# Two convolution layers on one core: rows of layer 1 loaded once, column filtering in a third chunk in a row, and three moved steps

## The chip, the core and the metric

The kernel runs on one core of a Trainium2 chip. The core has a matrix engine (PE), a vector engine (DVE), an activation engine (ACT), a general engine (POOL) and an engine that only issues transfers (SP). Each engine works through its own list of instructions in order; transfers between HBM and on-chip memory run on 16 DMA engines beside them. The metric is the device time of one execution in microseconds (us), the median of several runs. A change of up to 0.2% is taken as none.

## The reference

The input x has 8 images of 32 channels and 252 x 252 pixels, all float32. Two layers of the same form follow each other: a group normalization with 16 groups of two channels, a 5 x 5 convolution from 32 to 32 channels with reflected borders, and a residual sum. The reference writes the convolution as a product of Fourier transforms; with these paddings it is the plain convolution of the padded image.

```python
def _gn(v, G=16, eps=1e-5):
    B_, C_, H_, W_ = v.shape
    g = v.reshape(B_, G, C_ // G, H_, W_)
    m = jnp.mean(g, axis=(2, 3, 4), keepdims=True)
    s = jnp.var(g, axis=(2, 3, 4), keepdims=True)
    return ((g - m) / jnp.sqrt(s + eps)).reshape(v.shape)
...
x = x + _L0_conv_ref(_gn(x), L0_conv_weight)
x = x + _L1_conv_ref(_gn(x), L1_conv_weight)
```

## The kernel before

**Layout.** The 128 partitions hold 4 x 32: two column parities times two row parities of an image, times the 32 channels. A 5 x 5 convolution on the image is then a 3 x 3 convolution from 128 to 128 channels on an image of a quarter of the size. An image is cut into 8 chunks of 16 of these rows. The texts name a chunk (b, l, c): image, layer index (0 is layer 1, 1 is layer 2) and chunk. The normalization's scale is folded into the weights and its mean into a bias.

**Filtering.** Along the rows the kernel uses a filtering scheme with six points for four output rows. `transform` (L533) forms the points on DVE from sums and differences of rows: `row_pairs` (v, L562), `row_quads` (u, L571 and 572), `last_rows` (L578 and 579), then `point2` (L587), `point4` (L591), `point1` (L597), `point3` (L594) and `points05` (L604). In layer 2, `row_sums` (L544) gets v by DMA instead: POOL issues a copy (L552) and, when it has landed, two transfers that add to it (L554, L555). `conv` (L656) then multiplies: points 2 and 4 into the PSUM tiles m, points 1 and 3 into pairs (seeded by ACT from m, L724 and 726), points 0 and 5 into sums. Each product is three matmuls, one for each column of the 3 x 3 filter (L680). DVE and ACT combine the results to output rows: `evacuate` (L732), `difference` (L743), `inner` (L752, 753), `parts05` (L758, 759) and `outer` (L780).

**Column chunks.** In some chunks (`by_columns`, L961) points 0 and 5 are also filtered along the columns. DVE prepares sums and differences of columns (`columns`, L607: L613, L614, then L617 in layer 1 or L622 and 623 in layer 2), PE does eight short products instead of twelve passes of full length (`column_product`, L702, with a half-scaled copy L706 by ACT in between), and DVE puts the parts together (`column_parts`, L787 to 789).

**Order.** The chunks of layer 1 of image b + 1 alternate with those of layer 2 of image b (`order`, L946); image 0 begins alone and layer 2 of image 7 ends alone. Nothing is scheduled at run time: every step is entered in a table with a time of a hand-made clock, and each engine's list is the table in order of these times. `begin(i)` is the time at which chunk i starts on PE; a chunk takes 10.2 for its first four points, and `own` and `late` tell how much of points 0 and 5 is done in it and how much in the next. The times only set the order; waits are by semaphores.

**Loads.** `load` (L132, issued by SP) fetches the 16 rows of a layer-1 chunk into xs, in four quarters of 32 partitions. The two quarters of the other column parity hold the same pixels shifted by one. Where `once` (L161) holds, only two quarters are loaded, in two parts (2 rows and 14 rows), and `even_columns` (L156, at L159) copies them to the other half of the partitions, by ACT. `borders` (L145) fills the reflected columns on POOL: L148, 153 and 154, or L148, 150 and 151 where `once` holds. xs has two buffers. `once` holds in ten chunks: seven of image 0 and three of image 1.

**Rest.** ACT also forms the sums for the next image's statistics (`piece_sums`, L231 and 237) and the squares for layer 2's (`squares`, L855). `finish_stats` (L386) turns sums to scale factors by way of `variance` (L369, 371) and `inverse` (L377 to 383); `scale_points` (L511, ACT) and `add_residual` (L479, POOL) prepare the weights. `store` (L909) interleaves output columns into o (L917, by ACT, or by DVE in the last but one chunk) and `send_rows` (L896) lets SP write them; `store_half` (L930) does the last chunk.

Of the kernel before, what the change touches and what calls it, by code (L numbers as in the profile page):

```python
# [42 lines left out]
F32 = mybir.dt.float32  # L43
# [6 lines left out]
P = 128  # L50
# [6 lines left out]
def tile_conv_preact_x2(ctx: ExitStack, tc: tile.TileContext, x: bass.AP, w0: bass.AP, w1: bass.AP, out: bass.AP):  # L57
    nc = tc.nc
    B, C, H, W = x.shape
# [4 lines left out]
    ROWS = 4 * NT  # L64
    NCH = 8
    WIN = (NB + 2, NB + 3)
    WOUT = (NB, NB + 1)
# [8 lines left out]
    spool = ctx.enter_context(tc.tile_pool(name="spool", bufs=2))  # L76
# [15 lines left out]
    def at(t: float, fn, *args, **kw):  # L92
        table.append((t, len(table), fn, args, kw))
# [66 lines left out]

    def once(b: int, c: int) -> bool:  # L161

        return c < (NCH - 1, 3)[b] if b < 2 else False

    def parts(b: int, c: int):

        if once(b, c):
            return ((0, 10), (10, 6)) if (b, c) == (0, 0) else ((0, 2), (2, 14))
        return ((0, ROWS),) + (((ROWS, 2),) if c == NCH - 1 else ())
# [363 lines left out]
    def transform(t0: float, t1: float, b: int, l: int, c: int, free: float = -100.0, now=(0, 0, 0)):  # L533

        wi = WIN[l]
        got = {}

        def source():
            if l == 0:
# [4 lines left out]
        def row_sums(add: bool):  # L544

            t, nxt = source()
            if not add:

                i = max(order.index((b, l, c)) - order.index((B - 2, 1, NCH - 2)), 1 if (b, c) == (0, 1) else 0)
                got["v"] = vpool.tile([P, ROWS, wi], F32, tag=("va", "v")[i % 2], name=f"v_{b}_{l}_{c}")  # L550
                got["vt"] = got["v"].rearrange("p (t i) w -> p t i w", i=4)
                G.dma_start(got["v"], t)  # L552
            else:
                G.dma_start(got["v"][:, 0 : ROWS - 2], t[:, 2:ROWS], accum_op=ALU.add)  # L554
                G.dma_start(got["v"][:, ROWS - 2 : ROWS], nxt[:, 0:2], accum_op=ALU.add)  # L555

        def row_pairs(j0: int = 0, j1: int = NT):
            if j0 == 0:
                got["v"] = vpool.tile([P, ROWS, wi], F32, tag="v", name=f"v_{b}_{l}_{c}")
            v, (t, nxt) = got["v"], source()  # L560
            r0, r1 = 4 * j0, min(4 * j1, ROWS - 2)
            V.tensor_sub(v[:, r0:r1], t[:, r0 + 2 : r1 + 2], t[:, r0:r1])  # L562
            got["vt"] = v.rearrange("p (t i) w -> p t i w", i=4)

        def row_quads(j0: int = 0, j1: int = NT):
# [8 lines left out]
        def last_rows():  # L574

            u2, (t, nxt) = got["u"][:, 1], source()
            if l == 0:
                V.tensor_sub(got["v"][:, ROWS - 2 : ROWS], nxt[:, 0:2], t[:, ROWS - 2 : ROWS])  # L578
# [47 lines left out]
        if (b, l, c) == order[0]:  # L626
            at(t0 - 33.3, row_quads, 0, 2)
            at(t0 - 31, point2, 0, 2)
            for fn in (row_pairs, point4):
                at(t0, fn, 0, 2)  # L630
            at(t0 + 0.2, row_quads, 2, 4)
            at(t0 + 0.2, row_pairs, 2, 4)
            at(t0 + 0.2, last_rows)
            at(t0 + 0.2, point2, 2, 4)
            at(t0 + 0.2, point4, 2, 4)
            at(t0 + 4.9, point1)
            at(t0 + 5.5, point3)
            at(t0 + 6.2, points05)
        else:
            if l:  # L640
                two = begin(order.index((b, l, c)) - 2)
                at(two + 1.45, row_sums, False)
                at(two + 8.4, row_sums, True)
            else:
                at(t0, row_pairs)
            for dt, fn in ((2, row_quads), (3.2, last_rows), (3.6, point2)):
                at(t0 + dt, fn)
            at(max(t0 + 4.2, free + 9.45) if l else t0 + 4.2, point4)
# [244 lines left out]
        at(times[2], reflect)  # L893


    def send_rows(b: int, c: int, h: int, s: int, got):  # L896
        o = got["o"]
        for rp in range(2):
            r = 2 * (c * ROWS + 8 * h + 4 * s) - 1 + rp
            use = [i for i in range(4) if 0 <= r + 2 * i < H]  # L900
            if not use:
                continue
            i, m = use[0], len(use)
            q = 2 * s + rp
            S.dma_start(
                out[b, :, r + 2 * i : r + 2 * i + 2 * m - 1 : 2, :], o[q * Q : (q + 1) * Q, i : i + m, 1 : 1 + W]
            )

    def store(t0: float, b: int, c: int, got):  # L909
        copy = V.tensor_copy if (b, c) == (B - 1, NCH - 2) else A.copy  # L910

        def interleave(h: int, s: int):
            if s == 0:
                got["o", h] = opool.tile([P, 4, 2 * WOUT[1]], F32, tag="o", name=f"o_{b}_{c}_{h}")
            r, m = 8 * h + 4 * s, (3 if (c, h, s) == (NCH - 1, 1, 1) else 4)
            for cp in range(2):
                copy(got["o", h][halves[s], 0:m, cp::2], got["y"][halves[cp], r : r + m, :])  # L917

        def send(h: int):
            got["o"] = got.pop(("o", h))  # L920
            for s in range(2):
                send_rows(b, c, h, s, got)

        for i, t in enumerate((0, 3.3, 5.8, 7.8)):
            at(t0 + t, interleave, i // 2, i % 2)
        at(t0 + 4.6, send, 0)
        at(t0 + 9.1, send, 1)


    def store_half(t0: float, b: int, c: int, h: int, got):  # L930
        def interleave(s: int, rows: slice, engines):
            if (s, rows.start) == (0, 1):
                got["o"] = opool.tile([P, 4, 2 * WOUT[1]], F32, tag="o", name=f"o_{b}_{c}_{h}")
            for cp in range(2):
                dst, src = got["o"][halves[s], rows, cp::2], got["y"][halves[cp], 4 * s : 4 * s + 4][:, rows]
                eng = engines[cp]
                (eng.copy if eng is A else eng.tensor_copy)(dst, src)

        for s in range(2):
            eng = (A, A) if h or not s else (V, V)  # L940
            at(t0 - 0.2, interleave, s, slice(1, 3), eng)
            at(t0 + 1.4, interleave, s, slice(0, 1) if h and s else slice(0, 4, 3), (A, V) if h else eng)
            at(t0 + 1.4, send_rows, b, c, h, s, got)


    order = [(0, 0, c) for c in range(NCH)]  # L946
# [81 lines left out]
    for i, (b, l, c) in enumerate(order):  # L1028
# [11 lines left out]
        if i + 1 < len(order):  # L1040
            transform(t0 + (6.3 if i == 0 else 2.9), t1 + 0.2, *order[i + 1], free=t0, now=(b, l, c))
            nb, nl, ncx = order[i + 1]
            k = inputs.index((nb, ncx)) + 2
            if nl == 0 and 2 < k < len(inputs):
                for part in parts(*inputs[k]):
# [3 lines left out]
                    if once(*inputs[k]):  # L1049
                        kb, kc = inputs[k]  # L1050
                        t = 5.25 if part[0] == 0 and (kb, kc) != (1, 0) else 13.55 if kb else 8.5
                        at(t1 + t, even_columns, *inputs[k], *part)
# [71 lines left out]
```

## Time and profile before

| what | value |
|---|---|
| time, median of 3 runs | 1893.33 us (1890.24 to 1894.27) |
| the profiled execution: time, span | 1893.14 us, 1891.4 us |
| granted PE clock, mean | 0.994 |
| DMA queues: SP's (q1), POOL's (q0) | 272.09 MB, 135.28 MB |
| DMA share in 229 us of the middle (709 to 938 us) | 0.97 |
| DVE busy in the same 229 us | 213.05 us |
| ACT busy in the same 229 us | 178.36 us |

The profile comes from one execution, so sums are made against 1893.14 us. A group's row gives line, engine, operation, output and inputs, shape, the count, then busy time and mean ns of one, and behind the last bar the idle time of the engine just before these instructions with what ended it. A timeline row gives start and length in us, and in brackets the idle time before it. PEld is PE's weight load, which overlaps its matmuls.

### The profile page before, as it was taken

The page shows a single profiled execution, that of the slowest core. Times are in us where ns is not written, and L with a number is a line of the kernel's source. Part 1 is how long each engine was busy: PE and PEld are TensorE (multiplying, and loading weights), DVE is VectorE, ACT ScalarE, POOL GpSimd, SP SyncE. Part 2 cuts the span into 40 slices and gives each one's busy share as a digit, 9 for nine tenths or more (in the row PEclk, how much of TensorE's full clock was granted, in tenths as well). Part 3 has the DMA queues.
Part 4 walks back from the last instruction along what each step waited for, and adds up shares of the span by engine and source line. Part 5 has one row for each costly group of instructions (what it writes and reads, how often), then busy time and mean ns, then how long its engine had stood idle before and what let it go on. Part 6 is the DMA issues. An engine that isn't in the chain of part 4 may idle for free.

```text
span 1891.4 us, 20043 instructions
## 1 busy us (share of the span) xinstructions
PE 1851.5 (98%) x5162; PEld 956.7 (51%) x5162; DVE 1698.0 (90%) x2972; ACT 1401.1 (74%) x2695; POOL 372.9 (20%) x733
## 2 busy tenths in 40 slices
PE   5999999999999999999999999999999999999997
PEld 4444455545555555544555455555555545554455
DVE  7987899999998999999899898999989999998685
ACT  5887678778777787778787687877787765565665
POOL 4543211120112210131111310113111131111210
PEclk8999999999999999999999999999999999999999
DMA  9887899999999999999999989999999978995785
GB/s 278 205 176 191 201 248 230 212 229 253 219 239 239 206 249 233 212 244 219 246 224 229 220 214 258 221 227 226 215 260 220 236 184 177 193 203 145 192 217 113
DMA packets 248627, 411.41 MB, mean 218 GB/s; under 512 B 19520, under 2 KB 215488, under 8 KB 238144
## 3 DMA queue, kind: packets, MB, share of 16 engines
q1 hardware_dynamic: 220384, 272.09, 61.8%
q0 software_dynamic: 27648, 135.28, 28.7%
q10 hardware_dynamic: 480, 2.77, 0.4%
q8 instruction: 41, 0.67, 0.2%
q14 instruction: 74, 0.61, 0.1%
HBM read 207.41 MB, written 67.39 MB: 145 GB/s over the span
## 4 chain that ended last, share of the span: by engine, by line
PE 76%; DVE 9%; DMA 8%; ACT 3%; issue 2%; POOL 1%; SPq 0%; DVEq 0%; ACTq 0%; POOLq 0%
PE m L680 27%; PE pairs L680 26%; PE sums L680 8%; PE sums L702 6%; PE extra L702 6%; DMA v<-y 4%; PE extra L680 4%; DMA st<-in_x_dram 1%; DMA xs<-in_x_dram 1%; DMA out_dram<-o 1%; DVE sd L743 1%; ACT o L917 1%; DMA v<-ytail 1%; DVE t L604 1%; POOL u L479 0%
## 5 line engine op out<-in xcount | busy, mean ns | idle before, releaser
L680 PE MATMUL pairs<-t,u 128*128 128x504 f32 (+2 forms) x1548 | 690.4, 585 | 2.7 <-ACT pairs L726 1.6
L680 PE MATMUL m<-t,u 128*128 128x508 f32 (+3 forms) x1560 | 675.2, 581 | 7.1 <-DVE t L591 2.6
L680 PEld LDWEIGHTS m<-t,u 128*128 128x128 f32 x1560 | 293.3, 189 | 325.6 <-issue 297.4
L680 PEld LDWEIGHTS pairs<-t,u 128*128 128x128 f32 x1548 | 289.2, 189 | 321.5 <-issue 295.6
L917 ACT COPY o<-y 64x508 f32<-64x508 f32 x496 | 327.2, 660 | 8.9 <-DMA out_dram<-o 0.2
L743 DVE SCALAR_TENSOR_TENSOR sd<-sd,pairs 128x504 f32<-128x504 f32 (+2 forms) x258 | 163.9, 670 | 19.2 <-PE pairs L680 16.0
L680 PE MATMUL sums<-t,u 128*128 128x508 f32 (+5 forms) x408 | 175.3, 578 | 0.0
L855 ACT ACTIVATE junk<-y,negk 128x1008 bf16<-128x1008 f32 (+1 forms) x144 | 147.4, 1024 | 30.6 <-PE extra L702 14.9
L726 ACT COPY pairs<-m 128x504 f32<-128x504 f32 (+1 forms) x129 | 72.5, 562 | 129.6 <-PE m L680 110.0
L732 ACT COPY sd<-m 128x504 f32<-128x504 f32 (+2 forms) x258 | 137.0, 583 | 32.0 <-DVE sums L789 24.7
L604 DVE SCALAR_TENSOR_TENSOR t<-v 128x1024 f32<-128x1024 f32 (+1 forms) x128 | 157.5, 1230 | 3.5 <-PE sums L680 3.5
L702 PE MATMUL extra<-sdiff,wc 128*128 128x252 f32 (+3 forms) x616 | 156.3, 375 | 3.3 <-ACT extra L706 2.6
L702 PEld LDWEIGHTS extra<-sdiff,wc 128*128 128x128 f32 x616 | 113.5, 188 | 89.6 <-issue 50.2
L591 DVE SCALAR_TENSOR_TENSOR t<-v 128x512 f32<-128x512 f32 (+2 forms) x129 | 89.7, 695 | 65.6 <-DMA v<-y 47.7
L702 PE MATMUL sums<-d,u 128*128 128x252 f32 (+3 forms) x616 | 142.3, 373 | 0.0
L562 DVE TENSOR_TENSOR v<-xs 128x1792 f32<-128x1792 f32 (+1 forms) x65 | 129.5, 1993 | 1.8 <-issue 0.7
L554 POOL DMA_DIRECT2D v<-y x64 | 55.2, 863 | 377.7 <-DMA v<-y 377.7
L702 PEld LDWEIGHTS sums<-d,u 128*128 128x128 f32 x616 | 115.3, 189 | 26.9 <-issue 11.8
L237 ACT ACTIVATE st<-st,negk 128x1134 f32<-128x1134 f32 x98 | 121.7, 1242 | 3.2
L148 POOL COPY xs<-xs 64x32 f32<-64x32 f32 (+3 forms) x74 | 34.1, 461 | 450.2 <-DMA xs<-in_x_dram 330.7
L680 PEld LDWEIGHTS sums<-t,u 128*128 128x128 f32 x408 | 75.9, 188 | 80.1 <-issue 77.2
L231 ACT ACTIVATE st<-st 128x1134 f32<-128x1134 f32 x98 | 112.2, 1145 | 4.0 <-DMA st<-in_x_dram 2.8
(171 smaller groups left out, 2424.7 us busy)
## 6 DMA issues: line engine op xcount, KB each, us to landing
xs<-in_x_dram SPq DMA_DIRECT2D x176, 504.0 KB, 12.6
v<-y POOLq DMA_DIRECT2D x64, 1032.0 KB, 5.7
st<-in_x_dram SPq DMA_DIRECT2D x111, 567.0 KB, 6.9
out_dram<-o SPq DMA_DIRECT2D x488, 126.0 KB, 5.7
v<-y POOLq DMA_DIRECT2D x64, 903.0 KB, 9.9
u<-ud SPq DMA_DIRECT2D x15, 1152.0 KB, 5.6
xs<-in_x_dram SPq DMA_DIRECT2D x30, 441.0 KB, 6.7
xs<-in_x_dram SPq DMA_DIRECT2D x28, 472.5 KB, 11.1
```

The costliest lines, as they stand in the source:

```text
L231: A.activation(junk, src, AF.Identity, accum_out=acc[:, 0, i : i + 1])
L237: A.activation(junk, src, AF.Square, bias=negk, accum_out=acc[:, 1, i : i + 1])
L562: V.tensor_sub(v[:, r0:r1], t[:, r0 + 2 : r1 + 2], t[:, r0:r1])
L591: stt(ts[b, l, c][0][:, 1, j0:j1], vt[:, :, 1], -2.0, vt[:, :, 2], ALU.mult, ALU.add)
L604: stt(t, got["vt"][:, :, 0:2], 4.0 if l else -4.0, got["vt"][:, :, 2:4], ALU.mult, ALU.add)
L680: T.matmul(dst, u[:, k, 2 - i, :], rhs[:, j0 + i0 : j0 + i1, i : i + wo], start=(i == 0 and not add), stop=(i == 2), skip_group_check=add,)
L702: T.matmul(dst[:, 0, use], w, rhs[:, use], start=(i == 2), stop=True, skip_group_check=(i != 2))
L726: A.copy(dst, src)
L732: A.copy(got["sd"][:, 1 + e], m24[e][:, 0:n])
L743: stt(d, d, -2.0, pairs13[e][:, 0:n], ALU.mult, ALU.add)
L855: A.activation(dst, src, AF.Square, bias=negk, scale=1.0 if i else -1.0, accum_out=acc[:, 1, at_ : at_ + 1])
L917: copy(got["o", h][halves[s], 0:m, cp::2], got["y"][halves[cp], r : r + m, :])
```

## The change

There are five edits.

1. **Loads.** `once` holds in all chunks of layer 1 but the last of each image and chunk 1 (chunk 3 in image 1). The new ones are marked by `copied_late`: their two parts are loaded at the old place, and the borders and copies of the two parts have later times of their own. One copy of image 1 moves from 13.55 to 20.
2. **Columns.** `by_columns` takes chunk 2 of layer 2 in images 0 to 6 and chunk 3 in image 7.
3. **First chunk of layer 2.** (0, 1, 0) forms its v on DVE, as layer 1 does, with sums for differences. Only the later chunks of layer 2 use the transfers that add.
4. **Statistics of the last image.** `variance` and `inverse` of its layer 2 move from 12.82 and 13.55 to 11.3 and 12.5.
5. **The end.** o of the last but one chunk is taken from the pool of the statistics' pieces, and POOL issues its sends. Two sends of the last half chunk go to ACT's queue.

```diff
     def once(b: int, c: int) -> bool:
-        return c < (NCH - 1, 3)[b] if b < 2 else False
+        return c != NCH - 1 and (c != 1 if b > 1 else c != 3 if b else True)
+
+    def copied_late(b: int, c: int) -> bool:
+        return once(b, c) and (b > 1 or (b == 1 and c > 3))
...
+        sent = l == 1 and (b, c) != (0, 0)
...
-                i = max(order.index((b, l, c)) - order.index((B - 2, 1, NCH - 2)), 1 if (b, c) == (0, 1) else 0)
+                i = max(order.index((b, l, c)) - order.index((B - 2, 1, NCH - 2)), 0)
...
-            V.tensor_sub(v[:, r0:r1], t[:, r0 + 2 : r1 + 2], t[:, r0:r1])
+            (V.tensor_add if l else V.tensor_sub)(v[:, r0:r1], t[:, r0 + 2 : r1 + 2], t[:, r0:r1])
...
-            if l:
+            if sent:
                 two = begin(order.index((b, l, c)) - 2)
                 at(two + 1.45, row_sums, False)
                 at(two + 8.4, row_sums, True)
...
-            S.dma_start(
+            engines[rp].dma_start(
...
+        end = (b, c) == (B - 1, NCH - 2)
+        copy = V.tensor_copy if end else A.copy
...
-                got["o", h] = opool.tile([P, 4, 2 * WOUT[1]], F32, tag="o", name=f"o_{b}_{c}_{h}")
+                pool, tag = (spool, "st") if end else (opool, "o")
+                got["o", h] = pool.tile([P, 4, 2 * WOUT[1]], F32, tag=tag, name=f"o_{b}_{c}_{h}")
...
-                send_rows(b, c, h, s, got)
+                send_rows(b, c, h, s, got, (G, G) if end else (S, S))
...
-            at(t0 + 1.4, send_rows, b, c, h, s, got)
+            at(t0 + 1.4, send_rows, b, c, h, s, got, (S, A) if h and s else (S, S))
...
-        return c in {B - 1: (1, 2, 4, 5), B - 2: (1, 3)}.get(b, (1, 3, 5, 7))
+        return c in {B - 1: (1, 2, 3, 4, 5), B - 2: (1, 2, 3)}.get(b, (1, 2, 3, 5, 7))
...
+                    if copied_late(kb, kc):
+                        at(t0 + 9.5, load, kb, kc, *part)
+                        at(begin(i + 2) + 4.0 if part[0] else t1 + 5.5, borders, kb, kc, *part)
+                        at(begin(i + 3) + 4.0 if part[0] else t1 + 9.35, even_columns, kb, kc, *part)
+                        continue
...
-                        t = 5.25 if part[0] == 0 and (kb, kc) != (1, 0) else 13.55 if kb else 8.5
+                        t = 5.25 if part[0] == 0 and (kb, kc) != (1, 0) else (20.0 if kc == 2 else 13.55) if kb else 8.5
...
-            finish_stats(b, 1, *(te + t for t in (3.0 if b < B - 1 else 4.4, 6.85, 6.86, 10.25 if b else 9.9, 12.82, 13.55)))
+            finish_stats(b, 1, *(te + t for t in (3.0 if b < B - 1 else 4.4, 6.85, 6.86, 10.25 if b else 9.9, *((12.82, 13.55) if b < B - 1 else (11.3, 12.5)))))
```

More of the change, by code (lines that the diff above doesn't have):

```diff
@@ L576, in last_rows @@
             u2, (t, nxt) = got["u"][:, 1], source()
-            if l == 0:
-                V.tensor_sub(got["v"][:, ROWS - 2 : ROWS], nxt[:, 0:2], t[:, ROWS - 2 : ROWS])
+            if not sent:
+                (V.tensor_add if l else V.tensor_sub)(got["v"][:, ROWS - 2 : ROWS], nxt[:, 0:2], t[:, ROWS - 2 : ROWS])
             stt(u2[:, NT - 1], t[:, ROWS - 2], 4.0 if l else -4.0, nxt[:, 0], ALU.mult, ALU.add)
@@ L647, in transform @@
                 at(t0 + dt, fn)
-            at(max(t0 + 4.2, free + 9.45) if l else t0 + 4.2, point4)
+            at(max(t0 + 4.2, free + 9.45) if sent else t0 + 4.2, point4)
             at(max(t0 + 5.5, free + 7.8), point1)
@@ L893, in keep, with send_rows @@
         at(times[2], reflect)
-    def send_rows(b: int, c: int, h: int, s: int, got):
+    def send_rows(b: int, c: int, h: int, s: int, got, engines):
         o = got["o"]
@@ L909, in store @@
     def store(t0: float, b: int, c: int, got):
-        copy = V.tensor_copy if (b, c) == (B - 1, NCH - 2) else A.copy
+        end = (b, c) == (B - 1, NCH - 2)
+        copy = V.tensor_copy if end else A.copy
         def interleave(h: int, s: int):
             if s == 0:
-                got["o", h] = opool.tile([P, 4, 2 * WOUT[1]], F32, tag="o", name=f"o_{b}_{c}_{h}")
+                pool, tag = (spool, "st") if end else (opool, "o")
+                got["o", h] = pool.tile([P, 4, 2 * WOUT[1]], F32, tag=tag, name=f"o_{b}_{c}_{h}")
             r, m = 8 * h + 4 * s, (3 if (c, h, s) == (NCH - 1, 1, 1) else 4)
@@ L1044, in tile_conv_preact_x2 @@
             if nl == 0 and 2 < k < len(inputs):
-                for part in parts(*inputs[k]):
+                kb, kc = inputs[k]
+                for part in parts(kb, kc):
+                    if copied_late(kb, kc):
[3 more added lines that the diff above has]
+                        continue
                     early = once(*inputs[k]) or nb == 0
@@ L1048, in tile_conv_preact_x2 @@
                     at(t1 + (0.2 if early else 9.0), borders, *inputs[k], *part)
-                    if once(*inputs[k]):
-                        kb, kc = inputs[k]
-                        t = 5.25 if part[0] == 0 and (kb, kc) != (1, 0) else 13.55 if kb else 8.5
-                        at(t1 + t, even_columns, *inputs[k], *part)
+                    if once(kb, kc):
+                        t = 5.25 if part[0] == 0 and (kb, kc) != (1, 0) else (20.0 if kc == 2 else 13.55) if kb else 8.5
+                        at(t1 + t, even_columns, kb, kc, *part)
         if c == 0 and any(by_columns(b, l, k) for k in range(NCH)):
```

## The prediction

> **What bounds the kernel now.** I read the page's busy shares first, then its costliest groups, then the timeline.
>
> ```profile
> PE 1851.5 (98%) x5162; PEld 956.7 (51%) x5162; DVE 1698.0 (90%) x2972; ACT 1401.1 (74%) x2695; POOL 372.9 (20%) x733
> PEclk8999999999999999999999999999999999999999
> L680 PE MATMUL pairs<-t,u 128*128 128x504 f32 (+2 forms) x1548 | 690.4, 585 | 2.7 <-ACT pairs L726 1.6
> L680 PE MATMUL m<-t,u 128*128 128x508 f32 (+3 forms) x1560 | 675.2, 581 | 7.1 <-DVE t L591 2.6
> ```
>
> PE is busy 98% at full clock, and its two largest groups waited 10 us in all. Is it at its rate? [...]
>
> ```profile
> 904.36 5.23 PE L680 MATMUL m<-t,u 128*128 128x504 f32 x12
> 905.21 0.19 PEld L680 LDWEIGHTS m<-t,u 128*128 128x128 f32 x1 [0.23 <-issue]
> 905.63 0.19 PEld L680 LDWEIGHTS m<-t,u 128*128 128x128 f32 x1 [0.23 <-issue]
> 911.44 1.20 DVE L617 TENSOR_TENSOR d<-t 128x1008 f32<-128x1008 f32 x1
> 917.91 5.27 PE L680 MATMUL m<-t,u 128*128 128x508 f32 x12
> 929.85 5.23 PE L680 MATMUL m<-t,u 128*128 128x504 f32 x12
> ...
> 944.00 0.70 DVE L591 SCALAR_TENSOR_TENSOR t<-v 128x516 f32<-128x516 f32 x1 [4.20 <-DMA v<-y]
> 967.63 0.68 DVE L614 TENSOR_TENSOR sdiff<-t 128x504 f32<-128x504 f32 x1
> ```
>
> A weight load goes out every 0.42 us, which is what one pass of a matmul streams; the idle 0.23 us ends by "issue", not by data. [...] The same starts check the code's own clock: chunk (4,0,2) lasts 13.55, the plain (3,1,2) 11.94 with 3.4 us of its work put off into the next. By `own` and `late` (L966) a column chunk costs 13.6, a plain one 15.3, and between image edges the starts keep to this within 0.1 us. PE's schedule is the kernel's time; DVE is the near second. It has no idle over 0.2 us between 904 and 929, then 4.20 waiting for v.
>
> **Columns in eight more chunks.** `by_columns` gains chunk 2 of layer 2 in images 0 to 6 and chunk 3 in image 7. PE gains 15.3 - 13.6 = 1.7 each, **13.6 us**. DVE pays, start to start: columns (L613, 614, 622, 623) 2.52, column_parts (L787 to 789) 1.89, less 0.22 since the sums go to SBUF and not PSUM: +4.19. ACT pays one L706, 0.58, in a chunk that grows by 1.7.
>
> Is there room on DVE? Chunks 1, 2, 3 of layer 2 now stand in a row with layer-1 column chunks between. The tight consumer is the second half of PE's chunk, which reads sdiff (L614). In chunk (5,0,0), start 1077.08, L614 ended at 1085.81 and PE's extra matmul started at 1085.86 after 0.17 idle: the deadline is +8.61 us from a chunk's start. L614 of (4,0,2) ends at 911.53, +7.17. From there to L614 of (4,0,4), end 968.31, DVE takes 56.78; without the 4.20 wait and with 4.19 more work, 56.77. PE covers these four chunks in 54.41 instead of 56.11. So L614 lands at 7.17 + 56.77 - 54.41 = +9.53, **0.92 late**. The same sum on the other images (waits for v of 2.0 to 4.5 there) gives 0.8, 0.6, 0.9, 0.9, 0.9, 1.1 and, for image 6, whose L614 starts from +8.5, 2.0: 7.2 us. After that comes a plain chunk and the 3 us idle of chunk 5, so it is paid once per image. In image 7 no layer-1 work is beside it; L614 ends at +4.5 there and the 1.7 stays whole. Net **-6.4**.
>
> Is the v wait really free? v of (3,1,3) landed at 944.00, 26.1 after the start of (3,1,2). With the added work DVE reaches L591 at about +26.1 too, so the wait goes, and with fewer loads v should be no later.
>
> **Rows loaded once.** `once` grows from 10 chunks to 49. Each of the 39 drops two DMAs of 504 KB, some 40 of 411 MB. That brings no time directly: what waits for DMA is DVE,
>
> ```profile
> DVE t L591 <- DMA v<-y: 47.7, 17, 10.6
> ```
>
> and apart from the handover below PE does not wait behind it. The relief pays for the columns only. ACT gets two copies each (L159): 64x256, 0.42, and 64x1792, 1.86: 39 x 2.28 = 89 us. The long one is due at +4.0 of a layer-1 chunk. There ACT idles 1.88 us between its two seeds (L724 ends 907.75, L726 starts 909.63, waiting for PE), so the copy fits; L726 is 0.1 late, and its seed is used only at +7.65. The short one, +9.35, comes behind the L706 that PE waits for, in a chunk with 3.9 us of ACT idle. Behind both on ACT stand evacuations with over 1 us to spare. **0**; if the gap is missed, see the second rival. On SP the number of DMAs is the same and the loads keep their place. POOL's borders go from 3 copies a chunk to 6, at places where L552 has gone and the load, 12.6 us from issue, has landed.
>
> [...]
>
> ```profile
> L571 DVE SCALAR_TENSOR_TENSOR u<-y x64: 689/696/727, 176.1 to 1853.8; 128x516 f32<-128x516 f32 x64
> L151 POOL COPY xs<-xs x20: 179/202/2014, 30.2 to 164.6; 64x2 f32<-64x2 f32 x9, 64x14 f32<-64x14 f32 x9, 64x10 f32<-64x10 f32 x1, 64x6 f32<-64x6 f32 x1
> ```
>
> None lost more than 31 ns, while a 0.2 us POOL copy took up to 2.0: POOL is the one that waits. [...] I take 0.02 x 6 x 7 = **+0.8**.
>
> **Repairs.** Three stalls of PE stand in the trace.
>
> ```profile
> 189.62 0.70 DVE L591 SCALAR_TENSOR_TENSOR t<-v 128x516 f32<-128x516 f32 x1 [10.59 <-DMA v<-y]
> 190.46 2.79 PE L680 MATMUL m<-t,u 128*128 128x508 f32 x6 [2.05 <-DVE t L591]
> ...
> 1747.31 0.15 DVE L369 TENSOR_SCALAR var<-m 128x1 f32<-128x1 f32 x1
> 1747.52 3.67 PE L680 MATMUL m<-t,u 128*128 128x508 f32 x8 [2.08 <-DVE var L369]
> ...
> 1881.89 0.85 DVE L917 COPY o<-y 64x508 f32<-64x508 f32 x2 [4.25 <-DMA out_dram<-o]
> ```
>
> Chunk (0,1,0) takes its row sums on DVE. The 2.05 goes, and a 0.23 wait in the same chunk. But the 2.0 us row_pairs (L562, mean 1.993) is due at +2.9 of the chunk before, between var and inverse (+3.35), so rstd is ready at 178.0 instead of 176.2. The scaling L511 then starts 0.9 later (L159, moved from +13.55 to +20, no longer stands before it), and the seed L726 behind it with it: PE's wait of 1.38 at 178.61 grows by about 0.95. Net **-1.3**, between -2.3 and 0.
>
> In the last image's statistics var moves from 12.82 to 11.3, ahead of L743's second half, which waits for PE: it can run at 1742.9, when its matmul (1742.49) is done. The 2.08 goes: **-2.1**; nothing is late next, since inverse follows at 12.5 before L594.
>
> At the end, o of the last but one chunk comes from a free pool. L917 runs at 1877.7, not 1881.9. Then L743 waits for the pairs matmuls (end 1880.44) instead: L743 1881.0, L752 and L753 1881.7, the fourth L917 1882.6, L758 and L759 1883.3, L766 1883.9, L937 1884.6 against 1886.97. From there to the span's end took 4.4. The sends on POOL's queue are not in the trace: at L555's 1.2 us each, four after 1882.6 are issued by 1887.4 and land perhaps 2 later, about even with the last store. Bounds 0 to -3; I take **-2.0**.
>
> Sum: -6.4 + 0.8 - 1.3 - 2.1 - 2.0 = -11.0. The profiled execution took 1893.14 (span 1891.4); its 1882.1 is against the median 1893.33, 0.2 higher: **1882 us**. No change means within 0.2%, about 1889.5 to 1897.1, what this measurement can tell.
>
> **Rivals.** *No stall in the three chunks* (17%): DVE gets through, as its rows run a little faster with fewer POOL waits and transfers beside it; then 13.6 + 5.4 come whole: 1874. For it: 0.9 us late is 1.6% of 56.8. Against it: L613 to L623 do not wait for memory now.
>
> *The copies delay the seeds* (15%): if borders, queued on POOL behind L552's wait for L604, end late, the 1.86 us copy moves right. L726 with 0.6 must be done at +7.65, so the copy must start by +5.2, 1.8 after its gap opens. From 2.1 late it costs 0.28 in each of 39, 11 us in all, and the time is 1893, no change. Against it: POOL has a whole chunk of 13 us before that.
>
> [...]
>
> The forecast's own case, 1877 to 1888, has 50%; 9% lies between it and no change. The range 1873 to 1891 takes in the first rival and half of the way to the second. Faster 0.76, same 0.15, slower 0.09.
>
> **What would show it.** PE's chunk starts 13.6 apart through chunks 1 to 3; in chunk 4 a PE wait of 0.6 to 1.1 us before the extra matmuls, ended by DVE L614; L591's wait for v gone there; ACT's L726 still at +5.3; DMA share down by a tenth; no L591 wait near 189, no L369 wait near 1735; L917 without the DMA wait. Wrong would be PE waits ended by L726 in every layer-1 chunk, or L571 rows longer by tenths of a us.

## The result and the profile after

The changed kernel takes 1879.19 us (median of 4 runs, 1878.92 to 1884.91) against 1893.8 for the kernel before beside it (4 runs, 1890.24 to 1895.86): a ratio of 0.993, 95% interval 0.9915 to 0.9945. The forecast was 1882 with a range of 1873 to 1891. The profiled executions have spans of 1891.4 and 1877.5 us, 13.9 apart, where the forecast's sum was 11.0. The sum came near, but several of its terms did not: part of its nearness is luck, since errors of opposite sign made up for each other (below).

In the changed kernel's code the lines stand a little lower: L591 is now L596, L604 L609, L614 L619, L680 L685, L702 L707, L706 L711, L724 and 726 are L729 and 731, L917 is L925, L905 (the send inside `send_rows`) L910. The page after, the busy shares and PE's two largest groups:

```profile
PE 1839.2 (98%) x5194; PEld 966.0 (51%) x5194; DVE 1731.2 (92%) x3030; ACT 1493.8 (80%) x2781; POOL 396.2 (21%) x855
L685 PE MATMUL pairs<-t,u 128*128 128x504 f32 (+2 forms) x1548 | 692.9, 586 | 5.4 <-ACT pairs L729 3.3
L685 PE MATMUL m<-t,u 128*128 128x508 f32 (+3 forms) x1560 | 674.8, 581 | 3.4 <-DVE u L526 1.9
```

PE is busy 12.3 us less and still 98% of the span; DVE has 33 us more work and ACT 93. PE's waits moved from DVE (L591, var) to ACT (L729). POOL's queue moved 134.20 MB, 1.1 less than before (the first chunk of layer 2 no longer uses it for v), SP's 230.73 instead of 272.09.

The stretch that the forecast worked out, image 3's three column chunks, is here, from the timeline (start, length, idle before it). Chunk (4,0,1) starts at 871.43, (4,0,2) at 902.05, (4,0,4) at 956.50; L596 adds v into the fourth point, and L619 makes the sdiff that PE's extra products (L707) read:

```profile
883.58 0.70 DVE L596 SCALAR_TENSOR_TENSOR t<-v 128x516 f32<-128x516 f32 x1
907.41 0.68 DVE L619 TENSOR_TENSOR sdiff<-t 128x504 f32<-128x504 f32 x1
910.51 1.01 PE L707 MATMUL extra<-sdiff,wc 128*128 128x252 f32 x4
963.93 0.68 DVE L619 TENSOR_TENSOR sdiff<-t 128x504 f32<-128x504 f32 x1
964.95 0.37 PE L707 MATMUL extra<-sdiff,wc 128*128 128x252 f32 x1
```

L619 of (4,0,2) ends 6.04 after its chunk's start, and that of (4,0,4) at +8.11, half a microsecond before the +8.61 that the forecast gave as the deadline. PE does not wait. The kernel before, at the first two of these places (its chunk (4,0,1) starts at 873.74, (4,0,2) at 904.36):

```profile
887.21 0.70 DVE L591 SCALAR_TENSOR_TENSOR t<-v 128x516 f32<-128x516 f32 x1 [1.46 <-DMA v<-y]
910.85 0.68 DVE L614 TENSOR_TENSOR sdiff<-t 128x504 f32<-128x504 f32 x1
```

Before, DVE waited 1.46 us for v one chunk ahead of the stretch, and L614 ended at +7.17. That wait is gone after the change, and the three chunks begin 1.1 us earlier on DVE. Its cause is what the experiments were for.

To see where the 13.9 us came from, each chunk's start on PE is set against the code's own clock, and the lag's growth is read by stretch:

| part | forecast | measured |
|---|---|---|
| PE's own work, eight chunks, by the code's clock | -13.6 | -13.6 |
| stalls in the three column chunks | +7.2 | +0.8, all in image 0 |
| POOL's added copies, as time lost by DVE | +0.8 | not seen |
| handover, from the start of (1,0,0) to that of (0,1,2) | -1.3 | +0.6 (+2.4 in two other profiles) |
| var of the last image | -2.1 | -1.4 |
| the end, from the last chunk's start | -2.0 | -0.1 |
| the start, up to PE's first chunk | | +0.8 |
| turns from one image to the next | | -1.0 |
| sum | -11.0 | -13.9 |

The lag is how much later a chunk starts than the code's clock has it. Over the three column chunks of the changed kernel it stays within 0.05 us in images 1 to 6, which is how PE's own work is measured; the other rows are the change of the lag. Each profile is one execution. The turns cost 0.7 to 3.6 us an image over the profiles of this study (run 7 below aside), and which of them are long differs from one profile to the next; a difference of 2 us between two profiles means nothing by itself. The handover took 5.4 us before and 6.0 here, but 7.8 in runs 6 and 9 below, which have the same steps in this place: one profile each does not settle the size of this row.

### The profile page after: what moved, and what is told of

Same layout as the page of the kernel before. It is cut to its first block, busy times and chain, and to the rows that moved or that the text cites. A ratio compares the mean times of both kernels' runs of the same rounds, so it can differ in the third digit from the quotient of the medians.

```text
span 1877.5 us, 20381 instructions
## 1 busy us (share of the span) xinstructions
PE 1839.2 (98%) x5194; PEld 966.0 (51%) x5194; DVE 1731.2 (92%) x3030; ACT 1493.8 (80%) x2781; POOL 396.2 (21%) x855
## 2 busy tenths in 40 slices
DMA packets 207110, 369.07 MB, mean 197 GB/s; under 512 B 19088, under 2 KB 173968, under 8 KB 196752
## 3 DMA queue, kind: packets, MB, share of 16 engines
q1 hardware_dynamic: 178832, 230.73, 49.8%
q0 software_dynamic: 27600, 134.20, 29.3%
## 4 chain that ended last, share of the span: by engine, by line
PE 80%; DVE 7%; DMA 6%; ACT 3%; issue 3%; SPq 0%; POOL 0%; DVEq 0%; ACTq 0%; POOLq 0%
PE m L685 28%; PE pairs L685 28%; PE sums L707 7%; PE extra L707 6%; PE sums L685 6%; PE extra L685 4%; DMA v<-y 2%; DMA st<-in_x_dram 1%; DMA v<-ytail 1%; DMA xs<-in_x_dram 1%; ACT o L925 1%; DVE sd L748 1%; DVE t L609 1%; DMA wraw<-in_L_conv_weight_dram 1%; DMA out_dram<-o 0%
## 5 line engine op out<-in xcount | busy, mean ns | idle before, releaser
L685 PE MATMUL pairs<-t,u 128*128 128x504 f32 (+2 forms) x1548 | 692.9, 586 | 5.4 <-ACT pairs L729 3.3
L685 PE MATMUL m<-t,u 128*128 128x508 f32 (+3 forms) x1560 | 674.8, 581 | 3.4 <-DVE u L526 1.9
L685 PEld LDWEIGHTS m<-t,u 128*128 128x128 f32 x1560 | 294.2, 189 | 317.1 <-issue 297.0
L685 PEld LDWEIGHTS pairs<-t,u 128*128 128x128 f32 x1548 | 290.2, 189 | 320.1 <-issue 289.1
L925 ACT COPY o<-y 64x508 f32<-64x508 f32 x496 | 327.5, 660 | 8.6
L707 PEld LDWEIGHTS extra<-sdiff,wc 128*128 128x128 f32 x680 | 125.9, 189 | 98.1 <-issue 47.8
L707 PE MATMUL extra<-sdiff,wc 128*128 128x252 f32 (+3 forms) x680 | 173.0, 376 | 3.4 <-ACT extra L711 2.3
L557 POOL DMA_DIRECT2D v<-y x63 | 35.7, 567 | 622.7 <-DVE t L609 608.4
L609 DVE SCALAR_TENSOR_TENSOR t<-v 128x1024 f32<-128x1024 f32 (+1 forms) x128 | 157.7, 1232 | 5.4 <-PE sums L685 5.4
L707 PE MATMUL sums<-d,u 128*128 128x252 f32 (+3 forms) x680 | 157.4, 374 | 0.0
L707 PEld LDWEIGHTS sums<-d,u 128*128 128x128 f32 x680 | 127.6, 189 | 24.9 <-issue 9.0
L685 PE MATMUL sums<-t,u 128*128 128x508 f32 (+5 forms) x312 | 133.6, 577 | 0.0
L559 POOL DMA_DIRECT2D v<-y x63 | 54.3, 862 | 329.1 <-DMA v<-y 329.1
L159 ACT COPY xs<-xs 64x1792 f32<-64x1792 f32 (+2 forms) x97 | 109.3, 1129 | 13.4 <-POOL xs L151 11.1
L729 ACT ACTIVATE pairs<-m,means 128x504 f32<-128x504 f32 (+1 forms) x129 | 84.2, 653 | 44.5 <-PE m L685 36.0
L785 ACT ACTIVATE y<-sums 128x504 f32<-128x504 f32 (+1 forms) x158 | 94.5, 634 | 28.3 <-PE sums L707 19.2
L235 ACT ACTIVATE st<-st 128x1134 f32<-128x1134 f32 x98 | 112.5, 1148 | 5.0 <-DMA st<-in_x_dram 3.2
```

The source lines that it names most:

```text
L159: copy(t[64:128, :, 0:256:2], t[0:64, :, 1:256:2])
L235: A.activation(junk, src, AF.Identity, accum_out=acc[:, 0, i : i + 1])
L609: stt(t, got["vt"][:, :, 0:2], 4.0 if l else -4.0, got["vt"][:, :, 2:4], ALU.mult, ALU.add)
L685: T.matmul(dst, u[:, k, 2 - i, :], rhs[:, j0 + i0 : j0 + i1, i : i + wo], start=(i == 0 and not add), stop=(i == 2), skip_group_check=add,)
L707: T.matmul(dst[:, 0, use], w, rhs[:, use], start=(i == 2), stop=True, skip_group_check=(i != 2))
L785: A.activation(y, src, AF.Copy, scale=1.0 - 2 * i, **total(3 * i))
```

## The experiments

Each run's ratio is to the kernel before, timed on the same chip beside it (median 1894.46, 1893.76, 1892.56 and 1892.68 in the four groups).

**1. Columns alone.** Only `by_columns` is changed.

```diff
-        return c in {B - 1: (1, 2, 4, 5), B - 2: (1, 3)}.get(b, (1, 3, 5, 7))
+        return c in {B - 1: (1, 2, 3, 4, 5), B - 2: (1, 2, 3)}.get(b, (1, 2, 3, 5, 7))
```

> The kernel before with the column edit alone; loads, first chunk, statistics and end as before. Theory (the loads make the room): DVE enters the stretch of chunks 1 to 3 with the wait for v of chunk (b,1,1) still there (1.5 us at 886 us in the trace of before), so L614 of chunk 4 ends at about +9.5 us from its chunk's start, past +8.6, and PE waits 0.6 to 1.0 us before the extra matmuls in nearly every image: 5 to 7 us in all, and the time is 1885 to 1888. Rival (DVE had the room anyway, the forecast only mis-added): L614 at about +8.1, no waits, the whole 13.6 us come and the time is about 1880.

1890.97 us, ratio 0.9983 (0.9969 to 0.9998), 3.5 us faster by the median; 1885 to 1888 was expected, and only four of its ten runs (1886.34 to 1895.83), the profiled one among them, lie there. Its timeline in the same stretch (SPq and POOL rows are issues of transfers; chunks (4,0,1), (4,0,2), (4,0,4) start at 872.00, 902.78, 957.83):

```profile
870.49 2.26 SPq L143 DMA_DIRECT2D xs<-in_x_dram  x4
871.28 0.86 POOL L554 DMA_DIRECT2D v<-y  x1 [5.40 <-DMA v<-y]
885.83 0.69 DVE L591 SCALAR_TENSOR_TENSOR t<-v 128x516 f32<-128x516 f32 x1 [1.38 <-DMA v<-y]
909.48 0.68 DVE L614 TENSOR_TENSOR sdiff<-t 128x504 f32<-128x504 f32 x1
966.75 1.12 PE L702 MATMUL extra<-sdiff,wc 128*128 128x252 f32 x4 [0.31 <-DVE sdiff L614]
```

Here the forecast's picture is true: the wait for v stands, L614 of (4,0,2) ends at +7.38, and PE waits for L614 in (4,0,4) at +8.92. Over the three column chunks the lag grows by 0.8, 1.5, 1.2, 1.2, 1.3, 1.1 and 1.5 in images 0 to 6, 8.5 us where the forecast had 7.2; where the forecast put it all in (b+1,0,4), some of it falls in the chunk ahead. So the stall exists, and something else in the change takes it away.

**2. Loads alone.** `once`, `copied_late` and their loads, borders and copies; columns and repairs as before.

> The kernel before with the load edit alone (39 more chunks loaded once and copied by ACT, with their late borders and copies). Theory: no time for itself, within 2 us of before, while DVE's wait for v (L591, 47.7 us before) falls below 30 us and vanishes in chunk 1 of layer 1. Rival 1 (the copies cost ACT): slower by 2 us or more, PE waits ended by the seeds. Rival 2 (the lighter load cures the waits at image edges, 2.4 us of PE time in two of them before): faster by 2 to 3 us.

1891.35 us, 0.9986 (0.9975 to 0.9997). It brings some 3 us by the median, where none had been expected; its profiled execution took 1893.21, as long as that of the kernel before, so the trace does not say where they lie. What matters here it does show ((4,0,2) starts at 904.95):

```profile
886.53 0.69 DVE L596 SCALAR_TENSOR_TENSOR t<-v 128x516 f32<-128x516 f32 x1
910.32 0.68 DVE L619 TENSOR_TENSOR sdiff<-t 128x504 f32<-128x504 f32 x1
```

The wait for v in (4,0,1) is gone, and sdiff of (4,0,2) ends at +6.05.

**3. Repairs alone.** The row sums of (0,1,0) on DVE, the last image's statistics, the end.

> The kernel before with the three repairs alone (v of the first chunk of layer 2 on DVE, earlier variance of the last image, another buffer and other queues at the end). The forecast: -5.4 us, so 1888. From the trace after the change I now expect less: the first -1.3 becomes about +0.6, the second -1.4, the third -0.2, some -1 us in all, so 1892 to 1893, with PE's weight loads 0.84 us apart for a few us after its idle stretch in chunk (1,0,1).

1893.37 us, 0.9993 (0.9976 to 1.0009): no difference that this measurement can tell. The forecast gave these three 5.4.

**4. All, with the full bytes.** The changed kernel, but the late-copied chunks load all four quarters.

```diff
-        for cp, rp in quads[: 2 if once(b, c) else 4]:
+        for cp, rp in quads[: 2 if once(b, c) and not copied_late(b, c) else 4]:
```

> The changed kernel, but the late-copied chunks load all four quarters again, the other half being overwritten by ACT's copy with the same values. ACT, POOL and DVE do what they do after the change; only the 40 MB are back. Theory (bytes, not copies, decide when v lands and so whether DVE has room): the wait for v in chunk 1 returns with 1 to 2 us, L619 of chunk 4 ends past +8.6, PE waits 4 to 7 us more in all, time 1883 to 1886. Rival: as after the change, 1879.

1883.65 us, 0.9945 (0.9925 to 0.9964), with 409.34 MB instead of 369.07. The time lies within the 1883 to 1886 that was expected if bytes decide, but not for that reason: in images 1 to 6 the three chunks keep their start at +6.0 and no stall returns, and the 2.2 us that its profiled execution takes longer than the changed kernel's come in the turns between images. The two intervals overlap. So the saved bytes are not what gave DVE its room.

**5. Split loads without copies.** As run 4, and ACT's copies of these chunks are left out too, with borders for all four quarters. Of the load edit only the two parts (2 and 14 rows, eight transfers for four) and the later borders stay.

```diff
-        if once(b, c):
+        if once(b, c) and not copied_late(b, c):
...
-                        at(begin(i + 3) + 4.0 if part[0] else t1 + 9.35, even_columns, kb, kc, *part)
```

> The changed kernel, but the 39 chunks whose rows are loaded once load all four quarters again and are not copied on ACT; what stays of that edit is the load in two parts (2 and 14 rows, 8 DMAs instead of 4) and the borders filled later. Theory A (place in the queues): what gave DVE its room in the three column chunks is that the row adds no longer stand behind a load and its borders, not the bytes and not the copies. Then the first sdiff of chunk (b,0,2) ends +6.0 us after PE's chunk start, PE has no wait of over 0.2 us in chunk (b,0,4) of images 1 to 6, and the time is that of the run with all bytes loaded, 1881 to 1885 us. Theory B (the copies or the bytes): the start returns to +7.2 to +7.4, PE waits 0.3 us two to four times an image, and the time goes to 1887 to 1890.

1878.82 us, 0.9921 (0.9903 to 0.994), as fast as the changed kernel; the start is at +6.04 to +6.06 in images 1 to 6. The same 229 us of the middle by windows (length, busy time of PE, PEld, DVE, ACT and POOL, clock, DMA share, GB/s), first the changed kernel, then this one:

```profile
709.00:938.00 229.00, 228.77 (x647) 120.41 (x646) 219.78 (x378) 194.82 (x366) 42.91 (x94) 1.00 0.84 206
```

```profile
709.00:938.00 229.00, 228.79 (x649) 120.37 (x648) 219.70 (x378) 181.52 (x353) 46.25 (x94) 1.00 0.98 232
```

DMA share 0.84 or 0.98, ACT 195 or 182 us: PE has 228.8 of 229.0 in both. Loading the rows once saves traffic, costs ACT time, and gives this kernel nothing measurable; the split does.

**6. Split loads, borders early.** As run 5, with the borders of both parts at the place of before, so that POOL's order around the row adds is the old one.

```diff
-                        at(begin(i + 2) + 4.0 if part[0] else t1 + 5.5, borders, kb, kc, *part)
+                        at(t1 + 9.0, borders, kb, kc, *part)
```

> As the run with the split loads and no copies, but with the borders of both parts at their place of before, 9.0 us into the next chunk, so POOL's order around the row adds is that of the kernel before while the DMAs keep the split. Theory A1 (POOL's order: borders that wait for a load hold up the adds queued behind them): the start returns to +7.2 to +7.4 with PE waits of 0.3 us in chunk (b,0,4), time 1887 to 1890. Theory A2 (order on the DMA engines: the adds' data goes ahead of the load's): start stays at +6.0, no waits, 1881 to 1885.

1880.67 us, 0.9927 (0.9905 to 0.995); start at +6.04, no stall in images 1 to 6. POOL's order is not it. The same places of the timeline as in run 1:

```profile
869.44 7.90 SPq L143 DMA_DIRECT2D xs<-in_x_dram  x8
870.27 0.87 POOL L559 DMA_DIRECT2D v<-y  x1 [5.44 <-DMA v<-y]
883.30 0.69 DVE L596 SCALAR_TENSOR_TENSOR t<-v 128x516 f32<-128x516 f32 x1
```

POOL issues the adds 0.8 us after the load's first transfer in both. In run 1 two transfers of 504 KB stand ahead of the adds and the other two follow within 0.7 us; the adds' last packet ends 13.4 us after their issue. Here two or three of 63 KB stand ahead, the large ones come after, and the adds need 8.7. The changed kernel lies between: its load has 1 MB in four transfers, two of 63 KB and one of 441 KB ahead of the adds, the last 0.07 us behind, and they need 12.2:

```profile
869.68 1.78 SPq L143 DMA_DIRECT2D xs<-in_x_dram  x4
870.92 0.87 POOL L559 DMA_DIRECT2D v<-y  x1 [5.33 <-DMA v<-y]
```

That puts v there some 0.5 us before L596 asks for it. The packets show where the time goes: the adds are held back, not slowed. Their first packet starts 5.7 us after the issue in run 1, 4.8 in the changed kernel and 1.5 here; until then SP's queue moves 1.07, 0.85 and 0.18 MB. From the first packet to the last the adds take 7.6, 7.4 and 7.2 us, about the same in all three. Over images 1 to 6 the first packet comes 5.6 to 6.2 us after the issue in run 1, 1.5 to 4.9 in the changed kernel and 1.5 to 1.8 here. Why the first packet comes later where more of the load stands ahead, no run here shows.

**7. The load behind the adds.** Columns alone (run 1), with the whole load in four transfers but placed later on SP, behind the out sends.

```diff
-                    at(t0 + (14.0 if nb == 0 and part[0] == ROWS else 4.0 if early else 9.5), load, *inputs[k], *part)
+                    at(t0 + (14.0 if nb == 0 and part[0] == ROWS else 4.0 if early else 13.0), load, *inputs[k], *part)
```

> The kernel before with columns in five chunks alone (as the first run), and the load of a layer-1 chunk's rows placed 13.0 instead of 9.5 us into its chunk, behind the out sends on SP's queue and so behind the row adds that POOL issues at about +11; one whole load of 4 DMAs of 504 KB, no copies on ACT, borders where they were. Theory A (the load just ahead of the adds makes v late, and the wait for v in chunk (b,0,1) puts DVE 1.3 us back before the three column chunks): v's adds after (b,1,0) land in 8 to 10 us instead of 13, the wait of 1.4 us before the fourth point's sum in chunk (b,0,1) is gone, the first sdiff of (b,0,2) ends at +6.0, PE does not wait in (b,0,4), and 7 to 9 us are gained on the first run: 1881 to 1884 us. Theory B (it is something else in the split load): offset stays at +7.4 and the stalls stay, 1889 to 1893 us. A new wait by late borders would show on POOL, with v later than before.

1935.06 us, 1.023 (1.0211 to 1.0249): far slower, so the time that was expected failed. The mechanism did not. Rows of the timeline, in which (4,0,1) starts at 897.37 and (4,0,2) at 928.15:

```profile
909.73 0.69 DVE L591 SCALAR_TENSOR_TENSOR t<-v 128x516 f32<-128x516 f32 x1
933.54 0.68 DVE L614 TENSOR_TENSOR sdiff<-t 128x504 f32<-128x504 f32 x1
...
947.57 0.37 POOL L153 COPY xs<-xs 64x16 f32<-64x16 f32 x1 [5.40 <-DMA xs<-in_x_dram]
955.47 7.75 SPq L143 DMA_DIRECT2D xs<-in_x_dram  x4
956.34 0.86 POOL L554 DMA_DIRECT2D v<-y  x1 [7.29 <-DMA v<-y]
970.68 0.70 DVE L591 SCALAR_TENSOR_TENSOR t<-v 128x516 f32<-128x516 f32 x1 [4.18 <-DMA v<-y]
979.85 2.07 PE L702 MATMUL extra<-sdiff,wc 128*128 128x256 f32 x4 [2.19 <-DVE sdiff L614]
```

In (4,0,1) the adds took 9.2 us, with their first packet 1.4 us after the issue, the wait for v is gone and sdiff of (4,0,2) ends at +6.07, as in the changed kernel, with neither split nor copies. But the late load lands late. POOL's borders wait for it (L153 5.40 us here; L148 579 us over the whole kernel against 434 in run 1), and the row copy queued behind them goes out late, at 948.49. So its adds are issued at 956.34, behind the next load again; v is 4.2 us late and PE waits 2.2. A whole load costs time ahead of the adds, and at this place behind them too.

**8. Columns and loads, no repairs.**

```diff
-                        i = max(order.index((b, l, c)) - order.index((B - 2, 1, NCH - 2)), 0)
+                        i = max(order.index((b, l, c)) - order.index((B - 2, 1, NCH - 2)), 1 if (b, c) == (0, 1) else 0)
```

(The diff shows one line; the other repair edits are taken back likewise.)

> Columns in five chunks together with the rows loaded once and copied, and none of the repairs. Theory A (the two need each other: the split load takes away the wait for v in chunk (b,0,1), so that DVE enters the three column chunks 1.1 us sooner): first sdiff of (b,0,2) at +6.0, no wait of PE in (b,0,4), and together 11 to 14 us are gained where the two alone gained 3.5 and 2.7: 1879 to 1883 us. Theory B (the parts add up, and the rest came from the repairs): 3.5 + 2.7 = 6.2 us, about 1887.

1880.92 us, 0.9935 (0.992 to 0.9949): 11.8 us together where the two alone gave 3.5 and 3.1. The parts do not add up, they need each other. sdiff of (b+1,0,2) ends at +6.04 to +6.15 for images b = 1 to 6. Without the repairs the handover takes 8.6 us in its profile, against 5.4 in the kernel before and 6.0 to 7.8 in those with loads, columns and repairs.

**9. The last sends on SP.**

```diff
-                send_rows(b, c, h, s, got, (G, G) if end else (S, S))
+                send_rows(b, c, h, s, got, (S, S))
```

> The changed kernel, but the last-but-one chunk's eight sends go out on SP's queue as before and not on POOL's. Theory A (POOL's closing drain after sends of its own ends the kernel): no drain of 7 us, and the end is SP's last landing; from the start of the last chunk to the span's end 27 to 28 us instead of 29.7, time about 1877. Theory B (SP's queue is full at the end, so the last sends go out later): 29.5 to 31 us from that start, time 1879 to 1881.

1879.58 us, 0.9926 (0.9899 to 0.9954), no gain that can be told from the changed kernel. In the profile the end, from the last chunk's start to the span's end, is 28.9 us against 29.7 (before 29.8): 0.8, where 1.7 to 2.7 had been expected.

**10. row_pairs behind inverse.**

```diff
-                at(t0, row_pairs)
+                at(t0 + (0.6 if l else 0.0), row_pairs)
```

> The changed kernel, but the 2.0 us row_pairs of chunk (0,1,0) is put 0.6 us later in the order, behind inverse. Theory A (row_pairs between var and inverse makes the handover late, and the idle that it leaves on PE brings the half clock): rstd ends 1.9 us earlier, PE's wait of 2.07 near 180 falls under 0.7, no stretch of half clock follows near 182, and the lag from chunk (0,0,7) to (1,0,1) falls from 6.0 to between 3 and 4; time 1876 to 1877.5. Theory B (the handover is held by something else, such as the row's next needs): PE waits about as long at the row sums instead, and the time stays within 1 us of 1879.

1878.41 us, 0.9916 (0.9894 to 0.9938), by the times alone no gain clear of noise. PE's wait near 180 fell from 2.07 to 0.50 as expected, but the lag over the handover only from 6.0 to 4.5, not to under 4. The next wait, by the timeline (the expectation, and that of the next run, name the ends of this stretch by other chunks; the lag is taken from (1,0,0) to (0,1,2) throughout):

```profile
185.91 1.14 ACT L235 ACTIVATE st<-st 128x1134 f32<-128x1134 f32 x1
187.17 1.24 ACT L241 ACTIVATE st<-st,negk 128x1134 f32<-128x1134 f32 x1
192.79 0.65 ACT L729 ACTIVATE pairs<-m,means 128x508 f32<-128x508 f32 x1
193.58 5.35 PE L685 MATMUL pairs<-t,u 128*128 128x508 f32 x12 [3.03 <-ACT pairs L729]
```

ACT had no idle time over 0.3 us from 176.7 on, and the seed of pairs (L729) stands at the end of that row. In runs 6 and 9 the same wait is 3.04 and 3.02.

**11. A statistics piece later.** Runs 9 and 10 together, and ACT's piece 1 of image 2 (L235 and 241, 2.8 us) goes behind the seeds of (0,1,0).

```diff
-                        t = begin(NCH + (1, 1, 2, 2)[p]) + (9.8, 12.4, 9.8, 15.5)[p]
+                        t = begin(NCH + (1, 2, 2, 2)[p]) + (9.8, 8.8, 12.4, 15.5)[p]
```

> The changed kernel with the last sends on SP, row_pairs behind inverse, and ACT's statistics piece 1 of image 2 moved from chunk (1,0,1) into (0,1,0) behind the seeds (2.8 us of ACT). Theory A (after the two repairs ACT's backlog is what PE waits for in chunk (0,1,0)): PE's wait of 3.0 us ended by the seed of pairs near 194 falls to under 0.5, the lag from chunk (0,0,7) to (1,0,2) falls from 6.0 in the changed kernel to about 1.5, and with 0.8 from the end the time is 1873 to 1875 us. Theory B (the row's other needs take its place): lag stays over 3.5 and the time over 1876.

1872.38 us, 0.9896 (0.9882 to 0.9911), clear of the changed kernel's interval. PE's wait for L729 falls from 3.03 to 0.53, and the lag over the handover to 2.0 us (changed kernel 6.0).

**12. The end on SP and ACT.** Run 11, with the second half of the last-but-one chunk's sends by turns on SP and ACT.

```diff
-                send_rows(b, c, h, s, got, (S, S))
+                send_rows(b, c, h, s, got, (S, A) if end and h else (S, S))
```

> As the run with the piece moved, but the second half of the last-but-one chunk's sends goes on SP and ACT by turns. Theory A (SP's row of 22 sends at 0.43 us each sets the end, once POOL's drain is gone): four fewer on SP end the span about 1.5 us earlier, 27.4 us after the last chunk's start instead of 28.9; time 1 to 2 us under that run. Theory B (ACT's own copies of the last chunk come later behind its four sends): no gain, 28.5 to 30 us.

1870.55 us, 0.9891 (0.9874 to 0.9907), the lowest median here, though not clear of run 11; in the profile the end takes 28.0 us, 0.9 less than in run 11, where 1.5 had been expected. The closing drains of POOL and SP (count: shortest, median and longest in ns, then first and last start), first in the changed kernel, then here:

```profile
L1132 POOLq DRAIN  x3: 34/102/7252, 1869.5 to 1877.2; - x3
L1132 SPq DRAIN  x3: 7/7/7, 1874.2 to 1877.0; - x3
```

```profile
L1132 POOLq DRAIN  x3: 34/102/12377, 1824.5 to 1867.8; - x3
L1132 SPq DRAIN  x3: 7/7/7, 1867.3 to 1867.6; - x3
```

In the changed kernel POOL's long drain begins at 1869.5, when its last send is issued, and ends at 1876.7, 2.5 us after SP was done: it ends the kernel. Here it begins at 1824.5 and is over long before the end; SP's last sends set it.

## Why the prediction was right, and where not

**Right in its bound and its largest term.** PE's schedule was the kernel's time: the eight column chunks gave their 13.6 us within 0.2. Weight loads at 51% (51% after, too) said nothing of PE's room.

**The stall, "0.92 late", failed at its starting point.** The forecast took DVE's work between the two sdiffs as 56.77 us; it is 56.52. PE's 54.41 is 54.45. What was wrong is the "+7.17" at which the stretch begins. It was read from the kernel before and kept, while the wait of 1.46 us one chunk earlier, which made it, went away. The step behind it is that on the loads: "That brings no time directly", and "The relief pays for the columns only". Run 2 shows the start at +6.05 with the loads alone, run 1 shows +7.38 and 8.5 us of stall with the columns alone, and run 7 moves the start to +6.07 by the order of load and adds alone. So 7.2 of forecast stall were 0.8, all in image 0, whose start is at +7.0. This is the mechanism of the first rival (no stall), though not for its reason: L576 on y, L571 before, has a median of 697 ns against 696, so rows did not get faster.

**The reason given for the loads was wrong too.** "With fewer loads v should be no later" looked at the traffic. Runs 4 to 6 put all bytes back and keep the room on DVE, and run 7 gets it with neither split nor copies; what they share with the changed kernel is that less of the load stands ahead of the adds' first packet: SP's queue moves 0.1 to 0.9 MB between the adds' issue and that packet in images 1 to 6, against 1.1 to 1.3 in the kernel before and run 1. Whether half the bytes in one part would do as well was not tried.

**The handover, -1.3, was +0.6, in two other profiles +2.4.** That rstd would be late was foreseen: PE's wait for L731 was 1.38 and was to grow by 0.95, it became 2.07. What the step left out is what is late next. The L591 wait had covered ACT's row of copies and statistics; with it gone PE waits for L729, 1.27 us in the changed kernel and 3.0 in runs 6, 9 and 10. The forecast took the 2.05 from the kernel before; without the repair, but with columns and loads (run 8), that wait was 3.46, so the repair itself is not shown to be a loss. In the changed kernel the first wait was also followed by a stretch of half clock:

```profile
178.52 0.16 DVE L387 TENSOR_TENSOR rstd<-inv,fix 128x1 f32<-128x1 f32 x1
180.18 4.11 PE L685 MATMUL pairs<-t,u 128*128 128x504 f32 x6 [2.07 <-ACT pairs L731]
195.49 4.92 PE L685 MATMUL pairs<-t,u 128*128 128x508 f32 x11 [1.27 <-ACT pairs L729]
```

The window behind that wait, with a granted clock of 0.51 in its third column from the end:

```profile
181.50:185.00 3.50, 3.50 (x6) 1.64 (x5) 2.44 (x5) 3.45 (x4) 3.23 (x7) 0.51 0.94 149
```

Run 11, which removes both waits, shows that some 4 us lay in this place.

**The last image's var, -2.1, was -1.4.** The 2.08 went, but "nothing is late next" was wrong by 0.96: PE now waits for the seed L729 at 1739.1.

**The end, -2.0, was -0.1.** DVE and ACT did end earlier, by 2.6 us from the last chunk's start, as the step said. The step put POOL's sends as landing "about even with the last store" and had no row for POOL's drain behind them. Runs 9 and 12 get 0.8 and 1.7 of the 2.0 by taking the sends off POOL.

**The rival of delay, and POOL's copies.** L731 of (4,0,2) starts at +5.27, as in the kernel before, and PE's matmuls wait for L731 only in the handover (weight loads waited 0.35 us for it in three other chunks, and no matmul did): the copies delay nothing. No run shows the 0.02 us of the term 0.02 x 6 x 7. With POOL's L151 running 98 times instead of 20, L576 on y has a median of 697 ns (L571 before: 696) and a slowest row of 810 ns, and that one ran beside POOL's L483, not beside a copy: POOL's extra copies cost DVE nothing that can be read, and the +0.8 was not seen. That POOL is the one that waits, the kernel before shows at the two longest copies of L151, which end 0.07 us after the DVE instruction beside them:

```profile
58.59 2.07 DVE L562 TENSOR_TENSOR v<-xs 128x1792 f32<-128x1792 f32 x1
58.73 2.00 POOL L151 COPY xs<-xs 64x14 f32<-64x14 f32 x1
71.50 2.03 DVE L562 TENSOR_TENSOR v<-xs 128x1792 f32<-128x1792 f32 x1
71.59 2.01 POOL L151 COPY xs<-xs 64x14 f32<-64x14 f32 x1
```

The total came out 2.9 us below the forecast because a stall of 6.4 us that did not come outweighed repairs that fell short by 4.5; the start's 0.8 and the turns' 1.0 about cancel, and the 0.8 for POOL's copies makes up most of the rest. That errors of opposite sign cancelled this far was luck.

## What to carry to other kernels

A stretch's lateness is its work plus where it starts: when a change takes away a wait ahead of the stretch, the starting offset is a term of the sum and has to be worked out again. Where a transfer on the critical path is issued just behind a bulk load, cut the load so that most of it is issued after it (runs 1 and 6: 13.4 and 8.7 us for the adds); look at that order before counting bytes. For every stall that is repaired, follow the next consumer of each engine, and at the end of a kernel the closing work of each queue (here POOL's drain, 7.3 us), before the gain is booked.

## What was not expected of the hardware

**Half clock after two idle microseconds.** In the changed kernel 2.07 us of idle were followed by 3.41 us at half clock, and the six matmuls behind that wait took 4.11 us. In run 9 six behind a wait of 2.08 took 2.80, but nine behind a wait of 3.02 took 5.77; in run 10 twelve behind a wait of 3.03 took 5.35. So a wait of about the same length was sometimes followed by a slow stretch and sometimes not; what decides it, no run here shows.

**POOL's closing drain.** After issuing its last own transfer POOL drains for 7.3 us in the changed kernel, 10.9 in the kernel before and 12.4 in run 12. It is not only the wait for that transfer to land: the drain ends 5.1, 3.8 and 3.8 us after the last packet of POOL's queue. It costs nothing where POOL's last transfer is early, as in run 12.

**The same adds in 8.7 or 13.4 us.** Runs 6 and 1 move about the same bytes over the kernel; what differs is how much of the load had been issued by the time of the adds' issue. The difference is time before the adds' first packet, 1.5 or 5.7 us, not a slower move.
